# The second half of v in layer 1 from seven products of quarters, with paced first regroupings

## The chip, the cores and the metric

The kernel runs on one core of a Trainium2 chip. The metric is device time in microseconds, and less is better. All data is float32.

## The reference

There are two attention blocks over 8 images of 512 channels and 1024 tokens (32 by 32), each with 8 heads of 64 channels. The kernel changes here in the second, which reads the group-normalised output of the first:

```python
q = einsum('oc,bct->bot', w_q, xf).reshape(b, heads, hd, t)   # k and v likewise
attn = einsum('bhdq,bhdT->bhqT', q, k) * hd ** -0.5
attn = einsum('gh,bhqT->bgqT', w_head, attn)                  # heads are mixed
attn = softmax(attn, axis=-1)
attn = (attn - mean) / sqrt(var + EPS) * in_gamma + in_beta   # per image and head
out = einsum('bhqT,bhdT->bhqd', attn, v)
out = out.reshape(b, t, c) @ w_proj.T + b_proj
```

v is a product of a 512 by 512 matrix with 512 channels by 1024 tokens. The first block has the same projections (with a joint `qkv_w`), no mixing of heads, and a residual.

## The kernel before

**Layers and batches.** Layer 0 runs over the 8 images, then layer 1 does. An image is called a batch b. The order of the work on every engine is written out by hand: each engine executes its instructions in the order of the program text, and waits only where data or a buffer is missing. An `Agenda` holds small jobs by slot; the loop over steps calls `ag.run(slot)`.

**Projections by seven products.** In layer 0 all four projections, in layer 1 those for q, k and the output, multiply 2 by 2 blocks with seven block products instead of eight. The left factors (four blocks of the weights and three-or-four sums of them, seven in all, 1792 KB) are made once: `load_blocks` reads the blocks of a matrix, `combine_left` makes the sums on DVE and stores all seven in a DRAM tile `left_d`. The factors of layer 1's matrices are made during layer 0's first batches. The right factors are the blocks of the activations and four differences (`combine_right`). In layer 0, `project0` runs the products in the order 1, 2, 6, 5, 7, 3, 4; DVE adds the sums u2 and u3 in between, and `finish(i, j, x, y)` writes one quarter of the result (lines 938 to 944).

**v in layer 1.** `v_pair(b, i)` (line 1463) makes 256 tokens of v directly: 8 matmuls of 128 by 128 weights (tokens of y) against 512 columns of `wvT`, then one copy on ACT and one on DVE. Pairs 0 and 1 of the next batch run at the end of a batch. Pairs 2 and 3 run among the first scores of their own batch, in slots 1 and 3. For these, `load_wv_again` loads `wvT` once more, into the tile `z` of the sums of exponentials, which isn't needed there until step 5.

**A batch of layer 1** goes through half steps x = 0 to 36 (`half_step`). Each makes two tiles of scores (`scores`, line 1656; a PSUM tile of two banks, copied to `raw` by ACT or DVE), mixes heads for step x-4 (`mix`, line 1704), and adds the values for step x-5 (`values`, line 1750). Between scores and mix, eight DMAs of 256 KB each move a tile `raw` into `re` in another order (`regroup`, line 1680). The lists for the first two tiles (t=0, complete after x=1; t=1, after x=3) are issued at once; later pieces go out one at a time behind matmuls of mix and values. Mix needs t=0 at x=4 and t=1 at x=6. All tiles of scores, mixes and projections rotate through three PSUM tiles (`m_psum`). The first batch also runs three stages of group statistics (`group_stages`: means, squares, end), in slots 0, 1 and 3, and `v_sums` (line 1492) in slot 3.

**Between batches**: v pair 0 and 1, the output projection `out1` (line 1400, name pp), then `q_projection` (pq). `out1` uses two tiles of the pool `epool` ("e") for the residual `xs`, and sends each quarter out.

Names in the profile: `s` scores, `m` mix, `a` values, `pv` the products for v, `pq_p`, `pk_p`, `pv_p`, `pp_p` the products of layer 0 (all at line 902).

Of the kernel before, what the change touches and what calls it, by code (L numbers as in the profile page):

```python
# [18 lines left out]
P = 128  # L19
# [448 lines left out]
def tile_two_attention_layers(  # L468
# [29 lines left out]
    NR = 8  # L498
# [198 lines left out]
    with ExitStack() as l0:  # L697
# [21 lines left out]
        for c in range(NCC):  # L719
# [5 lines left out]
        HC = C // 2  # L725
        SOURCES = {
            "q": qkv_wT[:, 0:C], "k": qkv_wT[:, C : 2 * C], "v": qkv_wT[:, 2 * C : 3 * C],
            "p": proj_wT, "k1": wkT, "q1": wqT, "p1": w_projT,
        }
        left_d = {  # L730
            which: dram.tile([P, 7 * 2 * HC], F32, tag=f"left_{which}", name=f"left_{which}")
# [174 lines left out]
        def project0(nm, which, n, finish, by_token=False):  # L906


            left = left_t[which]
            b11, b12, b21, b22 = (n[:, 2 * i : 2 * i + 2, ts(j, FB)] for i in (0, 1) for j in (0, 1))  # L910
            s1, u2, s5 = tmp[4], tmp[5], tmp[6]

            def single(name):
                return [
                    ps_a.tile([P, FB], F32, tag="a0", name=f"{nm}_{name}_{i}", bufs=2)
                    for i in range(2)
                ]

            def double(name):
                t = score_psum(f"{nm}_{name}")  # L920
                return t, [t[:, 0], t[:, 1]]

            x = single("p1")
            product(x, left[:, 0], b11, True, by_token)
            for i in range(2):
                nc.scalar.copy(s1[:, i], x[i])
            product(x, left[:, 1], b21, False, by_token)
            finish(0, 0, x, None)
            t6, banks = double("p6")
            product(banks, left[:, 4], tmp[1], True, by_token)  # L930
            nc.vector.tensor_add(u2, s1, t6)
            t5, banks5 = double("p5")
            product(banks5, left[:, 3], tmp[0], True, by_token)
            nc.scalar.copy(s5, t5)
            t7, banks = double("p7")
            product(banks, left[:, 5], tmp[2], True, by_token)
            u3 = s1
            nc.vector.tensor_add(u3, u2, t7)
            product(banks5, left[:, 6], b22, False, by_token)
            finish(0, 1, t5, u2)  # L940
            finish(1, 1, s5, u3)
            x = single("p4")
            product(x, left[:, 2], tmp[3], True, by_token)
            finish(1, 0, x, u3)
# [256 lines left out]
        for b in range(B):  # L1201
            more = b + 1 < B
            ag = Agenda()
            ag.at(1, lambda: bias_xa(b))
            for c in range(NCC):
                ag.at(2 + 2 * c, lambda c=c: start_xa(b, c))
            for c, slot in enumerate((4, 7, 12, 15)):
                if b > 0:
                    ag.at(slot, lambda c=c: stats_out(b - 1, c))
                if more:  # L1210
                    ag.at(slot + 1, lambda c=c: load_x(b + 1, c))
            if b < 3:

                which = ("k1", "q1", "p1")[b]
                ag.at(1, lambda which=which: load_blocks(which, tag="junk"))
                for i, slot in enumerate((13, 14, 16, 17, 19)):
                    ag.at(slot, lambda which=which, i=i: combine_left(which, [i]))
            if more:
                stats0(b + 1, ag, 20)
                for c in range(NCC):  # L1220
                    ag.at(49 + 4 * c, lambda c=c: normalize0(b + 1, c))
                ag.at(32, lambda: load_left("k", b + 1))
                ag.at(33, lambda: load_left("v", b + 1))
            else:

                def load_first():
                    t = n_t["1"] = shared.tile([P, NCC, T], F32, tag="n", name="y_0")
                    for c in range(NCC):
                        nc.sync.dma_start(out=t[:, c], in_=x1_d[0][ts(c, P), :])

                ag.at(20, load_first)
                for slot, fn in zip((22, 25, 28), group_stages(0, B - 1, small_psum)):
                    ag.at(slot, fn)
                ag.at(32, lambda: load_left("q1", 0))
                ag.at(33, lambda: load_left("k1", 0))
                for c in range(NCC):
                    ag.at(49 + 4 * c, lambda c=c: normalize_to(n_t["1"][:, c], 0, c))
            attention0(b, ag)
            slot = NI + 2
            if more:  # L1240
                combine_right(f"{b + 1}", n_t[b + 1])
                qk0(b + 1, "k")
            else:
                combine_right("y1", n_t["1"])
                first_q1()
            ag.flush()
            if more:
                load_left("q", b + 1)
                v0(b + 1)
                load_left("p", b)  # L1250
                qk0(b + 1, "q")
            else:
                load_left("p", b)
                first_k1()
                first_wv()
            combine_right(f"{b}_xa", xa_t[b])
            out0(b)
            tmp.clear()
# [6 lines left out]
    with ExitStack() as l1:  # L1265
# [69 lines left out]
        def load_w(key, src, t):  # L1335

            w_t[key] = t.rearrange("p (c o) -> p c o", c=NCC)
            for c in range(NCC):
                nc.sync.dma_start(out=w_t[key][:, c], in_=src[ts(c, P)])
# [127 lines left out]
        def v_pair(b, i):  # L1467

            if i == 0:
                v_t[b] = shared.tile([P, NT, C], F32, tag="v", name=f"v1_{b}")  # L1470
            ps = m_psum(f"pv1_{b}_{i}")
            w = w_t["v", b]
            for m in range(2):
                for c in range(NCC):
                    nc.tensor.matmul(  # L1475
                        ps[:, m], y_t[b][:, c, ts(2 * i + m, P)], w[:, c],
                        start=(c == 0), stop=(c == NCC - 1),
                    )
            nc.scalar.copy(v_t[b][:, 2 * i], ps[:, 0])  # L1479
            nc.vector.tensor_copy(v_t[b][:, 2 * i + 1], ps[:, 1])  # L1480
# [158 lines left out]
        class Attention1:  # L1639
# [237 lines left out]
            def half_step(self, x, ag):  # L1877
                y, w = x - MLAG, x - MLAG - 1
                if 0 <= w < NX:
                    self.squares(w, 0)  # L1880
                    self.sum_e(w, 0)
                if x < NX:
                    self.scores(x, 0)
                if 0 <= w < NX:
                    self.squares(w, 1)
                    self.sum_e(w, 1)
                if x < NX + MLAG:
                    k_leave()
                if 0 <= w < NX:
                    self.sum_e2(w, 0)  # L1890
                    self.sum_e2(w, 1)
                k_leave()
                if 0 <= y < NX:
                    self.mix(y, 0)
                if 0 <= w < NX:
                    self.values(w, 0)
                if x < NX:
                    self.scores(x, 1)
                if 0 <= y < NX:
                    self.mix(y, 1)  # L1900
                if x <= MLAG or x >= NX:
                    self.regroup(n=NR)
                if x >= NX:
                    self.piece(n=len(self.pieces))
                ag.run(x - 0.5)
                if 0 <= w < NX:
                    self.values(w, 1)
                    self.e.pop(w)
                    if w % QLAG == QLAG - 1:
                        qb = w // QLAG  # L1910
                        self.leave(qb)
                        self.totals(qb)
                        if qb < NQB - 1:
                            ag.at(x + 2, lambda: self.reciprocals(qb, ag, x + 2))
                            ag.at(x + 6, lambda: self.divide(qb))
                ag.run(x)

        def load_wv_again(b):

            t = zpool.tile([P, 2, T], F32, tag="z", name=f"wv_{b}")  # L1920
            load_w(("v", b), wvT, t.rearrange("p j c -> p (j c)"))

        load_wv_again(0)

        NV = NT // 4
        for b in range(B):
            more = b + 1 < B
            a = Attention1(b)
            ag = Agenda()
            if b == 0:  # L1930
                for x, fn in zip((0, 1, 3), group_stages(B - 1, B, small_psum1)):
                    ag.at(x, fn)
            for i in range(NV):
                ag.at(1 + 2 * i, lambda i=i: v_pair(b, NV + i))
            if b == 0:
                ag.at(3, v_sums)
            free = (NX // 2 - 2 + b) % 2
            if more:
                a.pieces += [lambda i=i: y_piece(b + 1, i) for i in range(4 * NCC)]
# [43 lines left out]
            op = out1(b, right_o)  # L1983
            load_left(("q", b + 1))
            v_pair(b + 1, 1)
            load_wv_again(b + 1)
            op.run()
            q_projection(b + 1).run()

        top = stat.tile([P, 2], F32, tag="top", name="top")  # L1990
# [68 lines left out]
```

## Time and profile before

| | |
|---|---|
| median of 3 runs | 4238.78 us (4232.57 to 4243.62) |
| profiled execution | 4230.7 us, of which span 4228.9 us; clock 0.997 |
| PE busy | 4152.5 us, 98% |
| DVE busy | 2861.2 us, 68% |
| ACT busy | 2319.1 us, 55% |
| DMA queue of SP | 520.15 MB, 43.1% of 16 engines |

Layer 0 takes the first 1790 us or so, layer 1 the rest. A row of a group gives line, engine, operation, output and inputs, the count, busy time and the mean length of one record. Matmuls overlap, so the distance between starts in the timeline is what one costs, not its listed length. A float32 matmul leaves two records: a pair of v has 8 matmuls and 16 records.

### The profile page before, as it was taken

What the parts mean: (1) busy time and instruction counts of PE and PEld (TensorE: products, weight loads), DVE (VectorE), ACT (ScalarE), POOL (GpSimd) and SP (SyncE); (2) the same over time, 40 slices, a digit from 0 to 9 for tenths busy, and PEclk for the clock granted to TensorE, in tenths of its full rate; (3) what the DMA queues carried; (4) which work ended last, traced back from release to release, by engine and by line L of the source; (5) the groups of instructions that cost most, each with busy time, mean ns of one, the idle gap of its engine ahead of it and who ended that gap; (6) DMA issues with size and microseconds to landing.
All of it is one profiled execution on the core that took longest, in us unless ns stands there. A gap on an engine that the chain in (4) does not pass through costs nothing.

```text
span 4228.9 us, 131405 instructions
## 1 busy us (share of the span) xinstructions
PE 4152.5 (98%) x58572; PEld 2215.3 (52%) x58572; DVE 2861.2 (68%) x3779; ACT 2319.1 (55%) x2735; POOL 60.3 (1%) x86
## 2 busy tenths in 40 slices
PE   8999999999999999999999999999999999999998
PEld 4353535353535353456466466466466466466565
DVE  4748484848484747558668668568578588588587
ACT  2717171727272726259368278278277287286386
POOL 0000000000000000000000000000000000000000
PEclk9999999999999999999999999999999999999999
DMA  3212121212121212167467377277377376485575
GB/s 130 99 61 98 55 104 48 84 45 86 45 84 48 84 48 84 58 157 196 133 168 191 118 187 191 106 199 189 104 197 187 111 200 166 125 208 146 149 180 139
DMA packets 257905, 529.35 MB, mean 125 GB/s; under 512 B 52336, under 2 KB 59888, under 8 KB 250672
## 3 DMA queue, kind: packets, MB, share of 16 engines
q1 hardware_dynamic: 254752, 520.15, 43.1%
q8 instruction: 461, 7.55, 0.7%
q0 software_dynamic: 2576, 0.69, 0.4%
q14 instruction: 116, 0.95, 0.1%
HBM read 204.50 MB, written 46.92 MB: 59 GB/s over the span
## 4 chain that ended last, share of the span: by engine, by line
PE 92%; DVE 3%; DMA 2%; ACT 1%; issue 1%; SPq 0%; DVEq 0%; ACTq 0%
PE a L1750 12%; PE m L1704 11%; PE s L1656 11%; PE s L1082 10%; PE a L1108 10%; PE pv_p L902 5%; PE pp_p L902 5%; PE pk_p L902 5%; PE pq_p L902 4%; PE pk L1400 4%; PE pq L1400 4%; PE pv L1475 4%; PE pp L1400 3%; DMA re<-raw 1%; PE t L1781 1%
## 5 line engine op out<-in xcount | busy, mean ns | idle before, releaser
L1704 PEld LDWEIGHTS m<-wmix,re 64*64 64x64 f32 x32768 | 582.1, 135 | 120.7 <-issue 55.0
L1087 ACT ACTIVATE e<-s 128x1024 f32<-128x1024 f32 x512 | 497.2, 1026 | 234.4 <-PE s L1082 232.3
L1704 PE MATMUL m<-wmix,re 64*64 64x64 f32 x32768 | 592.2, 219 | 24.5 <-issue 17.7
L1710 ACT ACTIVATE e<-m 128x1024 f32<-128x1024 f32 x512 | 525.9, 1027 | 146.1 <-PE m L1704 142.6
L1728 DVE TENSOR_TENSOR z<-z,e 128x1024 f32<-128x1024 f32 x448 | 537.7, 1218 | 76.4 <-ACT e L1710 76.2
L1732 DVE TENSOR_TENSOR z<-z,e 128x1024 f32<-128x1024 f32 x448 | 534.1, 1219 | 62.1 <-ACT e L1721 60.4
L1750 PE MATMUL a<-e,v 128*64 128x256 f32 x4096 | 559.2, 393 | 3.1 <-issue 2.5
L1656 PE MATMUL s<-k,q 64*64 64x256 f32 x8192 | 553.6, 389 | 6.7 <-DVE q L1512 2.6
L1095 DVE TENSOR_TENSOR zacc<-zacc,e 128x1024 f32<-128x1024 f32 x384 | 468.6, 1220 | 82.6 <-ACT e L1087 61.0
L1671 ACT COPY raw<-s 128x1024 f32<-128x1024 f32 x368 | 372.9, 1013 | 267.9 <-PE s L1656 230.9
L1082 PE MATMUL s<-q,k 64*64 64x512 f32 x4096 | 490.1, 593 | 2.3 <-ACT e L1087 2.3
L1108 PE MATMUL a<-e,v 64*64 64x512 f32 x4096 | 484.1, 589 | 0.0
L1721 ACT ACTIVATE e<-e 128x1024 f32<-128x1024 f32 x448 | 460.0, 1056 | 0.0
L1656 PEld LDWEIGHTS s<-k,q 64*64 64x64 f32 x8192 | 268.3, 132 | 271.7 <-issue 167.5
L1750 PEld LDWEIGHTS a<-e,v 128*64 128x64 f32 x4096 | 251.4, 136 | 125.6 <-issue 17.3
L1108 PEld LDWEIGHTS a<-e,v 64*64 64x64 f32 x4096 | 156.7, 133 | 282.8 <-issue 282.5
L1082 PEld LDWEIGHTS s<-q,k 64*64 64x64 f32 x4096 | 147.9, 133 | 275.2 <-issue 241.4
L1669 DVE COPY raw<-s 128x1024 f32<-128x1024 f32 x144 | 175.9, 1221 | 97.4 <-PE s L1656 89.0
L1475 PE MATMUL pv<-wv,y 128*128 128x512 f32 x256 | 116.3, 608 | 0.3 <-DVE raw L1669 0.3
L1480 DVE COPY v<-pv 128x512 f32<-128x512 f32 x30 | 20.7, 689 | 139.3 <-ACT v L1479 139.3
L902 PE MATMUL pv_p<-left_v,tmp 128*128 128x256 f32 x512 | 113.1, 379 | 0.0
L902 PE MATMUL pq_p<-tmp,left_q 128*128 128x512 f32 x256 | 112.5, 592 | 0.0
(316 smaller groups left out, 4128.3 us busy)
## 6 DMA issues: line engine op xcount, KB each, us to landing
re<-raw SPq DMA_DIRECT2D x1024, 256.0 KB
rzb<-zd SPq DMA_DIRECT2D x256, 128.0 KB
left_q<-left_q SPq DMA_DIRECT2D x17, 1792.0 KB
left_p<-left_p SPq DMA_DIRECT2D x17, 1792.0 KB
left_k<-left_k SPq DMA_DIRECT2D x10, 1792.0 KB
x<-in_x_dram SPq DMA_DIRECT2D x32, 512.0 KB
x<-x SPq DMA_DIRECT2D x64, 256.0 KB
left_v<-left_v SPq DMA_DIRECT2D x8, 1792.0 KB
```

Source lines behind the costliest of these rows:

```text
L902: nc.tensor.matmul(out, st, mv, start=start, stop=(k == 1), skip_group_check=True)
L1082: nc.tensor.matmul(ps[c * D : c * D + D, m], k[r, hp, k0 : k0 + D], q[r, hp, ts(f, FB)], start=True, stop=True,)
L1087: nc.scalar.activation(e[i], ps, AF.Exp, scale=S0 * S0)
L1095: nc.vector.tensor_add(zacc[g], zacc[g], e[i])
L1108: nc.tensor.matmul(acc[g][a][m * D : m * D + D], v[rows, kc, ts(2 * hp + m, D)], e[i][rows, m], start=(kc == 0), stop=(kc == NG - 1),)
L1400: nc.tensor.matmul(self.ps[m][:, i], w[:, left, k * HC + i * P : k * HC + i * P + P], right[:, k], start=(k == 0 and m != 2), stop=(k == 1 ...
L1656: last = nc.tensor.matmul(pv[c * D : c * D + D, m, j], qo_t[b][r, 2 * qb + j, hp, ts(c, D)], k_t[b][r, hp, ts(kb, KB)], start=True, stop=True,
L1704: last = nc.tensor.matmul(ps[c * D : c * D + D, a, ts(r, D)], self.re[t, r][rows, j, k0 : k0 + D], wmix[rows].rearrange("p g i -> p (g i)" ...
L1710: nc.scalar.activation(self.e[y][:, j], ps.rearrange("p a c -> p (a c)"), AF.Exp)
L1728: nc.vector.tensor_add(self.z[:, j], self.z[:, j], self.e[y][:, j])
L1732: nc.vector.tensor_add(self.z2[:, j], self.z2[:, j], self.e2[j])
L1750: last = nc.tensor.matmul(self.acc[w][two * D : two * D + D, s].rearrange("p (c i) -> p c i", i=Q8), v_t[b][:, kc, ts(g, D)], e[:, g], sta ...
```

## The change

1. Layer 0 also makes the seven left factors of layer 1's `wvT` ("v1", in batch 2); those of the output projection move from batch 2 to batch 3.
2. In `project0`, `finish(1, 1)` moves ahead of product 3; it needs only sums in SBUF.
3. Pairs 2 and 3 of v in layer 1 are replaced by a class `SecondV`: the 512 tokens are two halves of 256, and seven products of two 256-channel halves by 256 tokens are made in four units: products 1 and 6 in slot 0, 2 and 7 in slot 1, 5 with 4, and 3, in slot 3. The left factors are loaded into the tiles `z` and `z2` with two DMAs; the four differences of y (`right`) are made by DVE in an `e` tile, after `out1` and ahead of `q_projection`.
4. For the first batch, `wvT` (for `v_sums`) is loaded into a half of `re`; the stages go to slots 0, 1 and 1.5, each after that slot's unit, and `v_sums` to slot 2.
5. The list of t=1 is no longer issued at once: five pieces go out at x=3, the other three behind the first three mixes.

```diff
-            "p": proj_wT, "k1": wkT, "q1": wqT, "p1": w_projT,
+            "p": proj_wT, "k1": wkT, "q1": wqT, "p1": w_projT, "v1": wvT,
...
             nc.vector.tensor_add(u3, u2, t7)
+            finish(1, 1, s5, u3)
             product(banks5, left[:, 6], b22, False, by_token)
             finish(0, 1, t5, u2)
-            finish(1, 1, s5, u3)
...
-            if b < 3:
-                which = ("k1", "q1", "p1")[b]
+            if b < min(B, 4):
+                which = ("k1", "q1", "v1", "p1")[b]
...
-                if x <= MLAG or x >= NX:
-                    self.regroup(n=NR)
+                if x < MLAG or x >= NX:
+                    self.regroup(n=NR if x != MLAG - 1 else 5)
...
-        load_wv_again(0)
+        class SecondV:
+            UNITS = ((1, 6), (2, 7), (5, 4), (3,))
+            def __init__(self, b):
...
+                for m, n in ((0, 4), (1, 3)):
+                    nc.sync.dma_start(
+                        out=t[m].rearrange("p j c -> p (j c)")[:, : n * W],
+                        in_=src[:, m * 4 * W : (m * 4 + n) * W],
+                    )
+            def right(self):
...
+                for i in range(4):
...
+                    nc.vector.tensor_sub(t[:, i], x, z)
+            def unit(self, n):
+                b = self.b
+                u, w = sums[0][:, 0], sums[1][:, 0]
+                ps = m_psum(f"pv1_{b}_{n}")
+                for i, m in enumerate(self.UNITS[n]):
...
+                    for h in range(2):
+                        for k in range(2):
+                            nc.tensor.matmul(
+                                ps[:, i, h * HC : h * HC + HC], right[:, k, ts(h, P)],
+                                self.left[f][:, k * HC : k * HC + HC],
+                                start=(k == 0 and h == 0), stop=(k == 1),
+                                skip_group_check=True,
+                            )
...
+                if n == 0:
+                    nc.scalar.copy(u, p[0])
+                    nc.vector.tensor_add(w, u, p[1])
+                elif n == 1:
+                    nc.vector.tensor_add(dst(0, 0), wide(u), wide(p[0]))
+                    nc.vector.tensor_add(u, w, p[1])
+                elif n == 2:
+                    nc.vector.tensor_add(dst(1, 1), wide(u), wide(p[0]))
+                    nc.vector.tensor_add(dst(1, 0), wide(u), wide(p[1]))
+                    nc.vector.tensor_add(w, w, p[0])
+                else:
+                    nc.vector.tensor_add(dst(0, 1), wide(w), wide(p[0]))
+        second_v = SecondV(0)
+        second_v.right()
+        load_w(("v", 0), wvT, re_t[:, 1, : NCC * C])
...
+            for slot, n in ((0, 0), (1, 1), (3, 2), (3, 3)):
+                ag.at(slot, lambda n=n, v=second_v: v.unit(n))
             if b == 0:
-                for x, fn in zip((0, 1, 3), group_stages(B - 1, B, small_psum1)):
-                    ag.at(x, fn)
-            for i in range(NV):
-                ag.at(1 + 2 * i, lambda i=i: v_pair(b, NV + i))
-            if b == 0:
-                ag.at(3, v_sums)
+                stages = group_stages(B - 1, B, small_psum1)
+                for slot, fn in zip((0, 1, 1.5), stages):
+                    ag.at(slot, fn)
+                ag.at(2, v_sums)
...
-            load_wv_again(b + 1)
+            second_v = SecondV(b + 1)
             op.run()
+            second_v.right()
             q_projection(b + 1).run()
```

More of the change, by code (lines that the diff above doesn't have):

```diff
@@ L1916, in half_step, with dst, wide @@
                 ag.run(x)
-        def load_wv_again(b):
-            t = zpool.tile([P, 2, T], F32, tag="z", name=f"wv_{b}")
-            load_w(("v", b), wvT, t.rearrange("p j c -> p (j c)"))
-        load_wv_again(0)
+        class SecondV:
+            UNITS = ((1, 6), (2, 7), (5, 4), (3,))
+            def __init__(self, b):
+                self.b = b
+                t = [
+                    zpool.tile([P, 2, T], F32, tag=f"z{m}", name=f"left_v{m}_{b}")
+                    for m in ("", "2")
+                ]
+                W = 2 * HC
+                self.left = [
+                    t[f // 4].rearrange("p j c -> p (j c)")[:, f % 4 * W : f % 4 * W + W]
+                    for f in range(7)
+                ]
+                src = left_d["v1"]
+                for m, n in ((0, 4), (1, 3)):
[4 more added lines that the diff above has]
+            def right(self):
+                y = y_t[self.b]
+                t = epool.tile([P, 2, T], F32, tag="e", name=f"right_v_{self.b}").rearrange(
+                    "p j (i t) -> p (j i) t", t=FB
+                ).rearrange("p f (k t) -> p f k t", k=2)
+                (self.b11, b12), (self.b21, self.b22) = (
+                    [y[:, 2 * i : 2 * i + 2, FB + j * QB : FB + (j + 1) * QB] for j in range(2)]
+                    for i in range(2)
+                )
+                for i in range(4):
+                    x, z = (
+                        (b12, self.b11), (self.b22, t[:, 0]), (self.b22, b12), (self.b21, t[:, 1])
+                    )[i]
+                    nc.vector.tensor_sub(t[:, i], x, z)
+                self.t = t
+            def unit(self, n):
[3 more added lines that the diff above has]
+                for i, m in enumerate(self.UNITS[n]):
+                    f, right = {
+                        1: (0, self.b11), 2: (1, self.b21), 3: (6, self.b22),
+                        4: (2, self.t[:, 3]), 5: (3, self.t[:, 0]), 6: (4, self.t[:, 1]),
+                        7: (5, self.t[:, 2]),
+                    }[m]
+                    for h in range(2):
[5 more added lines that the diff above has]
+                                skip_group_check=True,
+                            )
+                def dst(i, j):
+                    c = NT // 2 + 2 * j
+                    return v_t[b][:, c : c + 2, i * HC : i * HC + HC]
+                def wide(a):
+                    return a.rearrange("p (t o) -> p t o", o=HC)
+                p = [ps[:, i] for i in range(2)]
+                if n == 0:
[10 more added lines that the diff above has]
+                    nc.vector.tensor_add(dst(0, 1), wide(w), wide(p[0]))
```

## The prediction, made before the changed kernel ran

> **What bounds the kernel now.** I read the page first: shares of the engines, then the chain of waits by line, then the rows of the products concerned.
>
> ```profile
> span 4228.9 us, 131405 instructions
> PE 4152.5 (98%) x58572; PEld 2215.3 (52%) x58572; DVE 2861.2 (68%) x3779; ACT 2319.1 (55%) x2735; POOL 60.3 (1%) x86
> PE 92%; DVE 3%; DMA 2%; ACT 1%; issue 1%; SPq 0%; DVEq 0%; ACTq 0%
> L1475 PE MATMUL pv<-wv,y 128*128 128x512 f32 x256 | 116.3, 608 | 0.3 <-DVE raw L1669 0.3
> L902 PE MATMUL pv_p<-left_v,tmp 128*128 128x256 f32 x512 | 113.1, 379 | 0.0
> ```
>
> TensorE is busy 98% and makes 92% of the chain, so a microsecond of matmul taken out where it waits for nobody is a microsecond of time. The pairs to be replaced had almost no wait ahead of them (0.3 us in 256 records). Their own stage comes next: the timeline of PE at the start of batch 3 of layer 1.
>
> ```profile
> 2739.63 1.96 PE L1656 MATMUL s<-k,q 64*64 64x256 f32 x32
> 2741.96 1.96 PE L1656 MATMUL s<-k,q 64*64 64x256 f32 x32 [0.37 <-DVE q L1512]
> 2743.85 7.13 PE L1475 MATMUL pv<-wv,y 128*128 128x512 f32 x16
> 2750.91 3.70 PE L1656 MATMUL s<-k,q 64*64 64x256 f32 x64
> 2754.54 7.13 PE L1475 MATMUL pv<-wv,y 128*128 128x512 f32 x16
> 2761.60 1.09 PE L1656 MATMUL s<-k,q 64*64 64x256 f32 x16
> 2762.52 1.11 PE L1704 MATMUL m<-wmix,re 64*64 64x64 f32 x64
> 2768.13 0.46 PE L1704 MATMUL m<-wmix,re 64*64 64x64 f32 x15 [1.11 <-issue]
> ```
>
> By starts, a pair costs 2750.91 - 2743.85 = 7.06 us, two 14.12 us, and nothing else delays PE but 0.37 us for a PSUM tile. What limits the stage otherwise is the data of the first mix. Busy times and DMA by stretches of 4 us (the columns at the end are clock, DMA share, GB/s):
>
> ```profile
> 2748.00:2752.00 4.00, 4.00 (x27) 1.77 (x30) 0.36 (x1) 0.59 (x1) 0.00 (x0) 1.00 1.06 262
> 2752.00:2756.00 4.00, 4.00 (x53) 2.18 (x45) 2.69 (x3) 2.02 (x2) 0.00 (x0) 1.00 0.74 171
> 2756.00:2760.00 4.00, 4.00 (x11) 1.83 (x10) 0.00 (x0) 0.00 (x0) 0.00 (x0) 1.00 0.77 196
> ```
>
> SP issues t=0 from 2745.01, when ACT's last copy of x=1 is done; its eight pieces (2.1 MB) run at 223 to 275 GB/s (slices of 1.6 us) from about 2746.2 to 2754.6, so they land 9.6 us after the first issue. t=1 follows from 2756.5 to 2765. Then the waits of PE over the whole run (total, times, longest):
>
> ```profile
> PE m L1704 <- issue: 17.7, 24, 2.5
> PE m L1704 <- DMA re<-raw: 6.0, 10, 1.6
> PE s L1656 <- DVE q L1512: 2.6, 7, 0.4
> PE z L1127 <- DVE q L1018: 1.7, 1, 1.7
> ```
>
> "issue" is a wait for nothing that the profile shows. In batches 1 to 7 one falls in the 5 us after the first mix: 1.2, 2.5, 1.1, 2.2, 0.9, 1.5, 0.2, in all 9.6 us.
>
> [...] One record here steps by 217 ns at 256 columns (24.28 us for the 112 of v in layer 0, 666.86 to 691.14) and 441 at 512[...], so halving the columns halves the price. [...] 0.50 from 1812 to 1816 after PE had been busy 4.2 of 8 us. [...] the page shows 461 packets with 7.55 MB on such a queue. That it causes the issue waits behind bursts is my inference. [...]
>
> **Layer 1, batches 1 to 7.** Out: two pairs, 14.12 us. In: 7 products x 4 matmuls x 2 records = 56 x 0.217 = 12.14 us, priced by the same form in layer 0. The matmuls gain 1.98 us. Follow the PSUM tiles from the start of x=0 (clock 0 = 2739.63). Scores end at 1.9; unit 0 takes the third tile, which DVE's last q write frees at 2.2, so the 0.37 us wait stays; it ends at 5.8. ACT copies (0.59), DVE adds (0.69): tile free at 7.2. Scores of x=1 to 7.65, unit 1 to 11.1, its two adds to 12.5; scores of x=2 to 13.0, of x=3 to 14.8 (its second tile waits for a DVE copy that ends at 13.7, against 13.9: no wait); units 2 and 3 to 20.0; the first mix at 20.95 against 22.89 now. Gain 1.95 each, 13.6 us for seven.
>
> What this leans on. **t=0**: unit 0 sits ahead of x=1, so its issue moves from 5.4 to 8.8 while the first mix moves to 20.95; the room shrinks from 17.5 to 12.2 us, and the landing takes 9.6. Cover 2.6 us. **ACT's copy of x=4** waits for the same pieces (the raw tile is reused) and has about as much. **t=1**: five pieces from 16.0 are behind t=0, done by about 23.7; three more behind mixes at about 22, 24, 26, needed at 30. SP has nothing else queued behind these waits but y pieces of 0.3 us. **DVE** gains 4 differences and 7 adds less 2 copies, 9 x 0.68 = 6.1 us a batch, ACT loses 0.6; DVE is at 219 of 308 us and idle here for 7 us at a time. The differences wait until an output DMA frees an xs tile: the last-but-one finish is at 2714.3, landing near 2718.5, plus 2.7 us is 2721; the next DVE work of q is needed at 2722.6, and PE has three more products in hand even then. So nothing. **SP** issues two DMAs (1.79 MB) for four (1.05 MB) at 2686, behind left_q; at the 270 to 400 GB/s seen there, 2 to 3 us later end, and outputs start at 2703. Nothing. The first use is 55 us later.
>
> **Layer 0.** "v1" and the moved "p1" add 8 loads, a store and four DVE adds of 0.68 to batch 3. Batches with and without them now take the same: 214.48 us (427.31 to 641.79 with, 641.79 to 856.26 without). Nothing. `finish(1,1)` earlier: DVE's last two writes of a projection now follow each other with 1.33 us less backlog. Where q is followed by the output, PE waits 715.45 - 711.74 - 3.43 = 0.28 us: gone, 7 times, 2.0 us. k followed by z and v: z starts 0.3 sooner but v's tile comes free at the same moment (DVE can't start on bank 2 before PE ends): nothing, except batch 0 (0.3). First q of layer 1, with writes of 1.03 us each: z waits 1.73 and k 0.36; k's start moves from 1741.85 to about 1740.3: 1.6 us. Sum 3.9. It can't lose: PE's product 3 (3.43 us) covers the 1.2 + 1.4 (2.6 for the output).
>
> **Batch 0 of layer 1.** Here PE waits already, 1.4 + 2.4 + 0.7 + 0.4 + 0.3 us, and its clock halves.
>
> ```profile
> 1809.72 0.39 PE L622 MATMUL pm<-gs_m,gavg 128*128 128x4 f32 x2 [2.36 <-DVE gs_m L620]
> 1813.65 9.32 PE L1475 MATMUL pv<-wv,y 128*128 128x512 f32 x16
> 1835.01 4.06 PE L1492 MATMUL pvs<-ys,wv 128*64 128x8 f32 x128
> ```
>
> Now DVE does the differences (2.7) after its statistics (1808.2), then a raw copy and unit 0's add, then the means: pm waits 1.7. Squares stand behind unit 1's adds: pv waits 2.3. The end stage (3.1 us of small DVE work, 1827.8 to 1830.9) no longer runs beside a pair: v_sums waits about 3.6. I get the first mix at 1839.1 at full clock, against 1840.8, and put 3 to 4 us of slow clock on it: loss 1.5 us, bounds -1 (full clock) and +6 (slow through units 2 and 3).
>
> **Sum.** -13.6 - 3.9 + 1.5 = -16.0 us on an execution of 4230.7, -0.38%. That execution was 8 us faster than the median shown; I put the difference on the median: 4222.8. The issue waits are unbounded by this trace; I leave them at 9.6 in all. Bounds: none (-9.6) to 2 us more a batch (+14).
>
> **Rivals.** (1) **Issue waits grow**: units have 112 instructions for 64, and dense mixing starts 2 us sooner while DMAs are still full. Speaks for it: seven waits just there; against: pacing shortens the queue to 23.7. At 3.4 us a batch, +14: 4236.8. (2) **Late regrouping**, the one that ends slower: t=0 and the five of t=1 share the rings, 3.4 MB at 183 GB/s (171 and 196 in the stretches above) instead of 250 in turn: t=0 complete at 9.9 + 18.6 = 28.5, the first mix (last piece needed 21.9) 6.6 us late, 46 us for seven: 4268.8. It turns the result slower by over 0.3% from 4.1 us a batch. Against: t=0 and t=1 ran apart, and each at 250. (3) **Half the gain**: batch 0 costs its +6 and the DVE backlog wasn't what held layer 0: -13.6 + 6 = -7.6, 4231.2. That products are not fewer in time (weights bound) needs 252 ns a record; loads take 190: excluded.
>
> **Chances.** As forecast 0.55 (own range 4212 to 4226), (1) 0.20, (2) 0.15, (3) 0.10. A measurement of this kernel can tell about 0.3% (12.7 us): faster 0.55, same 0.30, slower 0.15. Range 4210 to 4248: below, no issue waits and a cheap batch 0 (-16 - 9.6 - 3); above, all of (1) and half of (2)'s lateness.
>
> **What would show it.** A row of 448 records with 256 columns for pv at 217 ns by starts; from the scores of x=0 to the first mix 20.9 us for 22.9; no DMA re<-raw wait at x=4; q to output 0.28 shorter; in batch 0 a wait of v_sums for ys of 3 us or more. Wrong: PE waits for re at the first mix, or issue waits over 20 us there.

## The result, and the profile after

The changed kernel takes 4221.55 us (median of 9 runs, 4216.58 to 4229.3) against 4241.38 us (9 runs) for the kernel before: ratio 0.9961, 95% interval 0.995 to 0.9972. A second session gave 0.9957 (0.9944 to 0.9971). The forecast was 4222.8 us. Its profiled execution has a span of 4214.8 us, 14.1 less than that of before. Line numbers up to 1900 hold for both kernels; the units are at 1972.

The page (shares, chain) and, from the groups by line, the rows that took the place of `pv<-wv,y`:

```profile
span 4214.8 us, 131897 instructions
PE 4139.5 (98%) x58764; PEld 2252.4 (53%) x58764; DVE 2916.2 (69%) x3855; ACT 2312.4 (55%) x2727; POOL 60.3 (1%) x86
PE 94%; DMA 2%; DVE 2%; ACT 1%; issue 1%; SPq 0%; DVEq 0%; ACTq 0%
L1972 PE MATMUL pv<-left_v,right_v 128*128 128x256 f32 x256 | 60.8, 386 | 0.2 <-DVE right_v L1957 0.2
L1972 PE MATMUL pv<-left_v,y 128*128 128x256 f32 x192 | 46.8, 387 | 2.8 <-PE s L1656 2.3 <-DVE raw L1669 0.5
L1957 DVE TENSOR_TENSOR right_v<-y 128x512 f32<-128x512 f32 x16 | 11.0, 685 | 4.4 <-DMA out_dram<-xs 4.4
```

There are the 448 records of 256 columns. PE's busy time fell by 13.0 us, nearly as much as the span; DVE's rose by 55 us, which costs something in batch 0 alone (below). The wait of the differences for an output DMA exists (4.4 us in eight batches) and holds nobody up.

The timeline of PE at the start of batch 3 of layer 1, as shown for before:

```profile
2734.43 1.96 PE L1656 MATMUL s<-k,q 64*64 64x256 f32 x32
2736.73 1.97 PE L1972 MATMUL pv<-left_v,y 128*128 128x256 f32 x8 [0.34 <-PE s L1656]
2738.53 1.89 PE L1972 MATMUL pv<-left_v,right_v 128*128 128x256 f32 x8
2740.35 1.96 PE L1656 MATMUL s<-k,q 64*64 64x256 f32 x32
2742.24 1.99 PE L1972 MATMUL pv<-left_v,y 128*128 128x256 f32 x8
2744.07 1.89 PE L1972 MATMUL pv<-left_v,right_v 128*128 128x256 f32 x8
2745.89 3.80 PE L1656 MATMUL s<-k,q 64*64 64x256 f32 x64
2749.62 3.72 PE L1972 MATMUL pv<-left_v,right_v 128*128 128x256 f32 x16
2753.18 1.89 PE L1972 MATMUL pv<-left_v,y 128*128 128x256 f32 x8
2755.00 1.09 PE L1656 MATMUL s<-k,q 64*64 64x256 f32 x16
2755.91 1.11 PE L1704 MATMUL m<-wmix,re 64*64 64x64 f32 x64
```

By starts, the units take 3.62 + 3.65 + 5.38 = 12.65 us for 14.12 of the pairs, and the first mix comes 21.48 us after x=0 (22.89 before): 1.41 us gained. No wait for `re` stands at the mix, and no issue wait follows it in this batch.

The waits of PE:

```profile
PE m L1704 <- issue: 14.5, 25, 1.4
PE m L1704 <- DMA re<-raw: 4.9, 9, 1.2
PE pv L633 <- DVE gs_sq L631: 3.1, 2, 2.3
PE s L1656 <- issue: 2.9, 2, 1.6
PE pvs L1492 <- issue: 2.7, 1, 2.7
```

Issue waits are shorter: those after the first mix of batches 1 to 7 fell from 9.4 to 4.9 us. The third line (2.3 of its 3.1 us) and the last are costs of batch 0 that were smaller or not there before. That `pvs` waited for `ys` is my reading of the timelines: DVE ended `ys` at 1822.26, `pvs` began at 1822.36. Batch 0 by stretches of 4 us (the third column from the end is the clock):

```profile
1812.00:1816.00 4.00, 2.11 (x10) 1.52 (x8) 1.75 (x5) 0.00 (x0) 0.00 (x0) 1.00 0.93 232
1816.00:1820.00 4.00, 3.33 (x34) 1.85 (x34) 2.05 (x9) 0.26 (x1) 0.00 (x0) 0.67 1.07 252
1820.00:1824.00 4.00, 1.64 (x32) 1.67 (x33) 1.95 (x15) 0.75 (x1) 0.00 (x0) 0.50 0.17 39
1824.00:1828.00 4.00, 4.00 (x79) 4.00 (x80) 0.00 (x0) 0.00 (x0) 0.00 (x0) 0.50 0.02 4
1828.00:1832.00 4.00, 4.00 (x54) 2.90 (x56) 0.88 (x2) 0.00 (x0) 0.00 (x0) 0.50 0.02 4
1832.00:1836.00 4.00, 4.00 (x23) 2.79 (x16) 0.57 (x1) 1.01 (x1) 0.00 (x0) 0.70 0.18 38
```

The clock is at half from 1817 to 1834, and full from there to 4206, almost the end of the run. `v_sums` takes 7.0 us for 4.06, the scores of x=3 3.6 for 1.9.

### The profile page after: what moved, and what is told of

It is laid out like the page before. It is cut to its first block, busy times and chain, and to the rows that moved or that the text cites. A ratio compares the mean times of both kernels' runs of the same rounds, so it can differ in the third digit from the quotient of the medians.

```text
span 4214.8 us, 131897 instructions
## 1 busy us (share of the span) xinstructions
PE 4139.5 (98%) x58764; PEld 2252.4 (53%) x58764; DVE 2916.2 (69%) x3855; ACT 2312.4 (55%) x2727; POOL 60.3 (1%) x86
## 4 chain that ended last, share of the span: by engine, by line
PE 94%; DMA 2%; DVE 2%; ACT 1%; issue 1%; SPq 0%; DVEq 0%; ACTq 0%
PE s L1656 12%; PE a L1750 12%; PE m L1704 11%; PE s L1082 10%; PE a L1108 10%; PE pk_p L902 5%; PE pq_p L902 5%; PE pv_p L902 5%; PE pp_p L902 5%; PE pk L1400 4%; PE pq L1400 4%; PE pp L1400 3%; PE pv L1972 2%; DMA re<-raw 1%; PE t L1781 1%; PE pv L1475 1%
## 5 line engine op out<-in xcount | busy, mean ns | idle before, releaser
L1093 DVE TENSOR_TENSOR zacc<-e,e 128x1024 f32<-128x1024 f32 x64 | 78.3, 1223 | 53.2 <-ACT e L1087 53.2
L902 PE MATMUL pk_p<-tmp,left_k 128*128 128x512 f32 x256 | 112.5, 592 | 0.0
```

The lines of the kernel that those rows point to most:

```text
L902: nc.tensor.matmul(out, st, mv, start=start, stop=(k == 1), skip_group_check=True)
```

## The experiments

Each ratio is to the kernel before, run in the same session. "Issue waits" below means those within 12 us after the first mix, summed over batches 1 to 7, from one profiled execution each.

**The moved finish, alone** (e1), in the kernel before:

```diff
+            finish(1, 1, s5, u3)
             product(banks5, left[:, 6], b22, False, by_token)
             finish(0, 1, t5, u2)
-            finish(1, 1, s5, u3)
```

> The kernel before with the move of finish(1,1) ahead of product 3 alone. Theory (less DVE backlog at the end of a projection): layer 0's period falls from 214.47 to about 214.1 us, q to output without its 0.28 us wait, first k of layer 1 about 1.6 us sooner; in all -4 to -5 us, ratio 0.999. Rival (the order of two DVE writes is free either way): periods of 214.47 stay, 0 us.

Ratio 0.9988 (0.998 to 0.9995). The period of layer 0 is 214.08 us. From the first product of k for batch 1 to the first v of layer 1 it took 1572.98 us (211.59 to 1784.57) against 1577.27 (212.84 to 1790.11): 4.3 us. The theory holds. In the timeline of this kernel, q is now followed by the output at PE's own pace (927.22 - 923.79 = 3.43; 3.72 before):

```profile
878.91 7.17 PE L902 MATMUL pv_p<-left_v,n 128*128 128x256 f32 x32 [0.27 <-DVE k L958]
923.79 3.60 PE L902 MATMUL pq_p<-tmp,left_q 128*128 128x512 f32 x8
927.22 7.03 PE L902 MATMUL pp_p<-xa,left_p 128*128 128x512 f32 x16
1736.40 7.13 PE L902 MATMUL pk_p<-y,left_k 128*128 128x512 f32 x16 [0.60 <-DVE q L1018]
```

Between k and v nothing is gained, as the prediction said: from the last product of k to the first of v it is 4.44 us in both (876.89 to 881.33 before, 874.47 to 878.91 here), now with a wait for DVE in it (the first line). DVE doesn't empty the last bank before PE has filled it: in the changed kernel, with the same move, it idles 0.96 us for PE ahead of the last write of k (878.86).

**The change without pacing** (e2).

```diff
-                    self.regroup(n=NR if x != MLAG - 1 else 5)
+                    self.regroup(n=NR)
```

> The changed kernel with all eight pieces of t=1 issued at once. Theory ([...] it took away the issue waits after the first mix): those waits return from about 3 us in batches 1 to 7 to about 9 us, +5 us over the changed kernel (ratio to before about 0.9973). Rival (the issue waits are luck of where a block of instructions ends): no change within 2 us, ratio 0.996.

Ratio 1.0008 (1.0001 to 1.0015): the whole gain is gone, some 20 us against the changed kernel, four times what the theory gave. Issue waits are 17.9 us (4.9 in the changed kernel, not the 3 of the expectation); no re wait at the first mix. The timeline in batch 3 shows one of them:

```profile
2765.14 1.08 PE L1750 MATMUL a<-e,v 128*64 128x256 f32 x8
2766.16 0.66 PE L1656 MATMUL s<-k,q 64*64 64x256 f32 x8
2768.68 0.66 PE L1656 MATMUL s<-k,q 64*64 64x256 f32 x8 [1.86 <-issue]
```

It breaks off in the middle of a group whose data are there. By stretches of 2 us of the same kernel, DMA had been full (share over 1.0) until 2765, 5 us into the dense work:

```profile
2761.07:2763.07 2.00, 2.00 (x109) 1.75 (x102) 0.30 (x1) 2.00 (x3) 0.00 (x0) 1.00 1.07 258
2763.07:2765.07 2.00, 2.00 (x104) 1.75 (x96) 1.12 (x2) 2.00 (x3) 0.00 (x0) 1.00 1.04 250
2765.07:2767.07 2.00, 1.75 (x28) 0.70 (x17) 1.11 (x2) 2.00 (x3) 0.00 (x0) 1.00 0.73 169
2767.07:2769.07 2.00, 0.39 (x8) 0.33 (x12) 1.23 (x1) 0.30 (x1) 0.00 (x0) 1.00 0.05 11
```

The waits themselves are not all. Two of the longest, and the stretches just behind them, in batches 1 and 2 (clock third from the end):

```profile
2146.40:2149.15 2.75, 0.00 (x0) 0.00 (x0) 0.00 (x0) 2.62 (x3) 0.00 (x0) 1.00 0.82 193
2150.36:2153.77 3.41, 3.41 (x62) 2.15 (x58) 2.68 (x3) 1.02 (x1) 0.00 (x0) 0.50 0.14 38
2456.83:2460.39 3.56, 0.00 (x0) 0.00 (x0) 1.33 (x2) 1.61 (x2) 0.00 (x0) 1.00 0.48 115
2460.97:2464.39 3.42, 3.42 (x30) 1.70 (x28) 1.23 (x1) 1.02 (x1) 0.00 (x0) 0.50 0.02 5
```

A third such stretch follows the wait of 3.10 us in batch 4 (3075.37 to 3078.79). PE is busy all through them at half clock; by my estimate, half of 3.4 us, each loses 1.7 us. Not every long wait brings one: 2.81 us in batch 7 didn't. The profile of the same changed kernel with pacing (e7, below) has none in batches 1 to 7. From the scores of batch 1 to those of batch 7 this run took 15.6 us more than e7: 9.0 are listed issue waits and 5.1, by that estimate, the three stretches at half clock.

**The first batch mended** (e3). `wvT` goes into the tile of left factors, so that `v_sums` needn't precede the regrouping of t=1; small DVE work goes ahead of long.

```diff
+        nc.vector.tensor_copy(gs.m, gs.mv[:, :, 0])
         second_v.right()
-        load_w(("v", 0), wvT, re_t[:, 1, : NCC * C])
+        left_tile(("v", 0))
+        w_t["v", 0] = w_t["v", 0][:, :NCC]
...
+            if b == 0:
+                ag.at(1, squares_dve)
             for slot, n in ((0, 0), (1, 1), (3, 2), (3, 3)):
...
-                for slot, fn in zip((0, 1, 1.5), stages):
-                    ag.at(slot, fn)
-                ag.at(2, v_sums)
+                ag.at(0, means_pe)
+                ag.at(1, squares_pe)
+                ag.at(1.5, stages[2])
+                ag.at(3, v_sums)
```

> The changed kernel with the order of the first batch mended: wvT for v_sums into the tile of left factors instead of re, so that v_sums can stand in slot 3 behind units 2 and 3; the copy of the means ahead of the differences; the DVE part of the squares ahead of unit 1's adds. Theory (batch 0 loses 5 us to three waits of PE, 1.6 + 2.3 + 2.7, and to the half clock they bring): waits nearly gone, clock 1.0 through slot 3, v_sums 4 us for 7; 8 to 11 us faster than the changed kernel, ratio to before 0.9935 to 0.994. Rival (the half clock comes from the wait at the change of layers and stays): only the waits go, 5 us, ratio 0.995.

Ratio 0.9933 (0.9919 to 0.9946). The stretch from the first v of layer 1 to the next k took 219.99 us (1783.42 to 2003.41), against 232.98 with the change and 226.78 (1790.11 to 2016.89) before. A second profile of the changed kernel (e7) has 228.75 (1783.29 to 2012.04), so the mending is worth 9 to 13 us, of which 8 to 11 were expected. The clock in these stretches stays full until `v_sums` is over (1.00 from 1812 to 1824, then 0.74 and 0.84 for 8 us), and `pvs` is back to 3.9 us. So the order in batch 0 made the long half clock, not the change of layers.

```profile
1819.49 1.89 PE L1972 MATMUL pv<-left_v,y 128*128 128x256 f32 x8
1821.31 3.91 PE L1492 MATMUL pvs<-ys,left_v 128*64 128x8 f32 x128
1825.15 1.31 PE L1656 MATMUL s<-k,q 64*64 64x256 f32 x16
```

**All units in slot 0** (e4), ahead of the scores of x=1:

```diff
-            for slot, n in ((0, 0), (1, 1), (3, 2), (3, 3)):
+            for slot, n in ((0, 0), (0, 1), (0, 2), (0, 3)):
```

> The changed kernel with all four units in slot 0, so that t=0 is issued about 9 us later and the first mix comes at the same time. Theory (t=0 needs 9.6 us to land, and the change used up most of the room): t=0 issued at about 17.8 us of the batch's clock, landed at 27.4, the first mix ready at 21.3 waits for re about 5 us in each batch, +35 to +42 us over the changed kernel, slower than before (ratio about 1.005). Rival (the regrouping has more room than counted, since mix takes the pieces one by one): under 1 us a batch, ratio 0.997 or less.

Ratio 1.0097 (1.0081 to 1.0112), slower: some 57 us over the changed kernel, where the theory gave 35 to 42. PE waits for `re` 42.9 us in all, about 5 a batch:

```profile
PE m L1704 <- DMA re<-raw: 42.9, 66, 2.3
PE m L1704 <- issue: 17.6, 27, 1.5
```

That is the late regrouping of rival (2), brought about: the cover that the prediction counted as 2.6 us was real and no wider than a few us. The theory left out the clock: in each of batches 1 to 7 it is at half for 6.8 to 10.2 us around these waits, by my estimate 18 us lost in batches 1 to 6 (half of PE's busy time in those stretches). The pieces arrive one per 1.04 us (mixes of 8 records start at 2771.74, 2772.80, 2773.84, 2774.87), 256 KB each, so about 251 GB/s. The four units in one group take 2762.64 - 2750.39 = 12.25 us, for 12.65 in three groups.

**Pacing alone** (e5), in the kernel before:

```diff
-                if x <= MLAG or x >= NX:
-                    self.regroup(n=NR)
+                if x < MLAG or x >= NX:
+                    self.regroup(n=NR if x != MLAG - 1 else 5)
```

> The kernel before with the pacing of t=1 alone (five at x=3, three behind the first mixes). Theory (issue waits after the first mix come from instruction blocks that queue with the regrouping, so pacing helps the old kernel too): the 9.4 us of issue waits there fall to 2 or 3 us, and the time by 6 to 9 us, ratio 0.998. Rival (pacing only gives back what the earlier start of mixing costs, since the old kernel's burst ends by itself 3 us into the mixing): no change within 2 us.

Ratio 0.9976 (0.9967 to 0.9986); issue waits 1.8 us for 9.4. The theory holds: by these ratios over half of what the change brings can be had without a single product fewer. With the moved finish (e1) it would be nearly all, if the two add: 0.9988 x 0.9976 = 0.9964. No run has both.

**The changed kernel again** (e7), in the session of e5, e8 and e9.

> The changed kernel as it is, for a comparison in the same session with the others. Ratio to before 0.996 (0.995 to 0.997), some 12 to 20 us above the kernel with the first batch mended (e3).

Ratio 0.9957 (0.9944 to 0.9971), issue waits 5.4 us.

**A load more** (e10). In batches 1 to 7, behind the five pieces of t=1:

```diff
+            def extra():
+                left_tile(("extra", b))
+                nc.sync.dma_start(out=..., in_=left_d["v1"][:, :1536])
+            if b:
+                ag.at(2.5, extra)
```

> The changed kernel with one load more in batches 1 to 7: 768 KB of the factors of v, as much as the three held-back pieces, into the idle tile of left factors, issued at x=3 right behind the five pieces of t=1; nothing reads it. Theory (the issue waits after the first mix are instruction blocks that queue with any transfer): issue waits there grow from about 5 us in seven batches to 12 to 18, as without pacing, with no re waits to speak of; ratio to before 0.9985 to 1.001. Rival (pacing helps through the regrouping itself, its order or its buffers): under 7 us of issue waits, ratio 0.996.

Ratio 1.0004 (0.9996 to 1.0013), issue waits 19.2 us, a little over the 12 to 18 expected, re waits as before (5.1 us in the run). 768 KB that nobody reads cost about the same as the three unpaced pieces of e2 (17.9 us of issue waits, ratio 1.0008), so here it is bytes in the queue as mixing starts, not the regrouping.

```profile
PE m L1704 <- issue: 22.9, 27, 3.1
PE s L1656 <- issue: 8.9, 3, 3.4
PE m L1704 <- DMA re<-raw: 5.1, 13, 0.8
```

**What the issue waits wait for.** The page lists a queue of packets of kind "instruction", q8 (before: the 461 packets and 7.55 MB of the prediction); the traces hold the start and end of each packet. It carries 16 KB a packet, 462 in the changed kernel, one for every 255 of PE's instructions in the trace. In the twelve traces, `s`, `m` and `a` of layer 1 have 394 issue waits of over 0.15 us. If PE's instructions (matmuls, weight loads and those of its sequencer) are counted through in runs of 256, all 394 end at the same place of a run (number 193 or 194), and the latest q8 packet had landed 1.2 to 1.9 us earlier. I read this as PE waiting there for its next block of instructions: an engine waits not only where data or a buffer is missing, since in these 394 places the profile shows neither. What differs between the runs in batch 4 is the start of the packet, not its transfer. In the median of e7 a packet starts 1.1 us after PE has begun the block before it. For the wait in batch 4 it started 2.5 us after that in e7, 3.9 in e2 and 4.1 in e10, each packet then took 1.1 to 1.3 us, and PE waited 1.69, 3.10 and 3.26 us.

**Pacing further, on top of the mended first batch**: four pieces at x=3 (e8), units 0 and 1 behind the scores of x=1 and x=2 in batches 1 to 7 (e9), both (e11):

```diff
-                    self.regroup(n=NR if x != MLAG - 1 else 5)
+                    self.regroup(n=NR if x != MLAG - 1 else 4)
...
-            for slot, n in ((0, 0), (1, 1), (3, 2), (3, 3)):
+            for slot, n in ((1 if b else 0, 0), (2 if b else 1, 1), (3, 2), (3, 3)):
```

> e3 with four pieces of t=1 at x=3 instead of five, so that four go out behind mixes and the first values. Theory (every 256 KB less in the queue when mixing starts is about 1 us less delay for instructions): the issue waits after the first mix fall from about 5 us in seven batches towards 2, and the ratio from 0.9933 to about 0.9925. Rival (with five the queue is short enough; the last piece now comes close to its use at x=6): no change within 2 us, or re waits of 0.3 us a batch.

> e3 with units 0 and 1 in slots 1 and 2 in batches 1 to 7, behind the scores of x=1, so that t=0 is issued 3.6 us sooner, as in the kernel before. Theory (what matters at the start of mixing is what is still queued): t=0 lands before t=1 is issued, the five pieces are through about 2.5 us sooner relative to the first mix, issue waits there go to 1 us or less; ratio about 0.992. Rival: the waits that are left have other causes, same as e3 within 2 us.

> e9 (first batch mended, units 0 and 1 one slot later in batches 1 to 7) with four pieces of t=1 at x=3. Theory: with t=0 landed before t=1 starts there is under 1 us of issue waits left to win, so the same as e9 within 2 us, ratio 0.992. Rival (each piece less still counts over the rest of the batch): 3 to 5 us faster, ratio 0.9915.

Ratios 0.9923 (0.991 to 0.9937), 0.9924 (0.9911 to 0.9938) and 0.9935 (0.992 to 0.995). The issue waits fell from 5.0 us (e3) to 1.8, 0.8 and 2.1, near what the theories of e8 and e9 have (that 256 KB less in the queue is 1 us less delay was an estimate; a piece took 1.04 us in e4), but the times aren't told apart from e3 or from each other. All four, e3 included, lie about 0.7% below the kernel before, and below the changed kernel's 0.9961 and 0.9957.

## Why the prediction was right, and where its sum was not

Total: -16.0 us forecast, -14.1 between the two profiled executions and -0.39% (0.28% to 0.5%, 12 to 21 us) in the timed runs. The bound was PE and the path went through the matmuls, as argued. But three terms were off and partly cancelled, so that the total came this near is in part luck.

- **Units, -13.6 forecast, -9.9 measured** (7 x 1.41). The mis-sized term is 56 x 0.217 us: that price was read from a long row of 112 records, and each of the three groups cost about 0.17 us more at its ends (12.65 us for 12.14; 12.25 in one group, e4). The pairs too carry it: 7.06 us for 16 records at 0.429, where the prediction read 0.441 a record with the ends spread over them. PSUM tiles and copies fell in place as worked out: the wait of 0.37 us stayed (0.34), t=0 went out 8.98 us after x=0 began (forecast 8.8).
- **Issue waits, 0 forecast, about -4 to -4.5 measured** (9.4 to 4.9, and 5.4 in e7), and some -3.4 of clock with them, by my estimate half of two stretches: before, the clock was at half for 3.4 us behind the waits of 2.45 us in batch 2 and 2.24 us in batch 4 (2459.8 to 2463.2, 3077.6 to 3081.0); the changed kernel's two profiles have no such stretch. The prediction kept the waits at 9.6 for want of evidence and had no term for their clock. The runs show two effects against each other: the units without pacing, which start the mixing sooner and the regrouping later, take them to 17.9 (e2), pacing brings them down. Rival (1) is true of the change without its pacing: in e2 the waits reached 17.9 of the 23.6 us that it priced, and the whole gain went.
- **Batch 0, +1.5 forecast, +6.2 measured** (226.78 to 232.98), just past its upper bound; in e7, the same kernel, it was +2.0 (228.75). The waits themselves were sized well (forecast 1.7, 2.3, 3.6; measured 1.6, 2.3, 2.7). The term for the slow clock was wrong. Its 3 to 4 us were my estimate, no more than in the kernel before: there the granted clock was 0.50 from 1811.28 to 1818.11, behind 8 us in which PE was busy for 4.2, and again for 3.4 us behind `v_sums`. In the changed kernel it was at half for some 17 us (10 us in e7), which cost `v_sums` 3 us, the scores of x=3 1.8 and unit 2 0.8. It returned only at about 1834, 5 us after `v_sums` ended: through the 7 us of `v_sums`, matmuls of 8 columns, it stayed at 0.50, though the profile lists PE as busy there. My term had nothing for that. In the profile of before, too, half clock stands beside `v_sums`: it ran from 1835.01 to 1839.08 with no wait ahead of it, and the clock went to half at its end (two stretches of 3.4 us of that profile, clock third from the end):

```profile
1835.17:1838.59 3.42, 3.42 (x122) 3.42 (x122) 0.69 (x1) 0.54 (x1) 0.00 (x0) 1.00 0.99 232
1838.59:1842.00 3.41, 3.41 (x76) 2.67 (x77) 0.23 (x1) 0.90 (x1) 0.00 (x0) 0.50 0.04 10
```

- **Layer 0, -3.9 forecast, -4.3 measured** (e1). "v1" and "p1" cost nothing that stands out: in the run without pacing the period is 214.08 with "v1" (425.06 to 639.14), 214.08 with "p1" (to 853.22) and 214.09 with neither (to 1067.31). The batch with "v1" took 214.72 in the changed kernel's own profile, 214.08 to 214.39 in the other runs that have it.

These terms sum to -15.9 us, with -4.5 for the waits, where the two spans differ by 14.1; the other 1.8 us isn't placed.

Rival (2) did not happen in the change: in its trace PE has 0.00 us of idle time ahead of the first mix in each of batches 1 to 7. That t=1 stays behind t=0 in the queue was an estimate, which no run shows by itself. e4 shows how near the rival was: 9 us later costs 5 us of waits a batch, and 8 in all. Rival (3) was half true, in batch 0 only. The upper end of the range is mis-summed: all of (1) and half of (2)'s 46 us would be 4222.8 + 14 + 23, about 4260, not 4248.

What stays open: why one wait of 3 us is followed by half clock and another isn't (2.81 us in e2 and 3.43 us in e10 were not), and whether the moved finish and the pacing add up. The figures by stretch come from one profile a kernel, and batch 0 of the same kernel differed by 4 us between two of them.

## What to carry to other kernels

Before moving dense instruction work earlier, look at what DMA has in its queue at that moment. Here 768 KB that nobody reads took the waits that the profile calls "issue" from 5.4 us (e7) to 19.2 (e10) in seven batches, and behind waits of 2.75, 3.56 and 3.10 us the clock stood at half for 3.4 us each (e2), though not behind one of 2.81. Hold back the pieces that aren't needed yet. Price small groups with their ends, from a group of the same size: the three groups of units cost 12.65 us for 12.14. And don't count a stretch of tiny matmuls as busy when you judge the clock: in the changed kernel 7 us of them, at 8 columns, left it at 0.50.

## What the runs showed of the hardware that I had not expected

768 KB more in SP's queue as TensorE goes into its densest stretch cost about 0.45% of the whole time (e10 to e7), at a DMA share of 0.63 on average over these batches. In batch 4 the packet of instructions started 4.1 us after PE had begun the block before it, for 2.5 in e7, and all 394 issue waits of `s`, `m` and `a` over 0.15 us stand at one place of a run of 256 instructions, 1.2 to 1.9 us behind the landing of a packet. A group of matmuls between groups of another shape cost some 0.17 us above its records (12.65 us for 12.14 in three groups). And 128 matmuls of 8 columns, in which PE is listed as busy, went with half clock: it stayed at 0.50 for all of their 7 us in the changed kernel, and where they ran at full clock in 3.9 to 4.1 us, with no wait ahead of them, 3.4 us at half followed in before and e3, but not in e9 and e11.
